# Slots of a sparse edge bucket given out from both ends, in a four-layer graph network on one core

## The chip, the core and the metric

The kernel runs on one NeuronCore of one Trainium2 chip. Its time is the device time of one launch, in microseconds (us); the time before is the median of three runs. One more execution was recorded by the hardware profiler, and every duration below is from that one.

A core has TensorE (PE, matrix products into PSUM), VectorE (DVE), ScalarE (ACT), GpSimd (POOL) and SyncE (SP). Each works through its own list of instructions in a fixed order and waits for the others by semaphores. SP computes nothing here: it issues the kernel's transfers (DMAs).

## The reference

Sixteen graphs of 1024 nodes with 128 features go through four residual layers, each of which starts with a layer norm and a ReLU. The adjacency is sparse and its pattern symmetric: an entry is there with a chance of about 1.6%, and the diagonal is full. Layers 0 and 1 are a mean over neighbours and a linear map; layer 3 is an attention over the neighbours. The change is in layer 2, which runs two rounds of this:

```python
a = jnp.einsum('bnd,de->bne', x, We1[l, :D])
b = jnp.einsum('bnd,de->bne', x, We1[l, D:])
h = jax.nn.relu(a[:, :, None, :] + b[:, None, :, :] + be1[l])
scores = jax.nn.sigmoid(jnp.squeeze(h @ We2[l], -1) + be2[l])
upd_adj = adjacency * scores
messages = jnp.einsum('bnm,bmd->bnd', upd_adj, x)
```

A score is needed for each pair of nodes (n, m), but it counts only where the adjacency isn't zero.

## The kernel before, in words

**Buckets.** The kernel computes h only for the pairs that are edges. The 1024 nodes are eight blocks of 128. A bucket is the set of edges between block t and block u: 28 outer buckets (t < u) and 8 on the diagonal. Each edge of a bucket gets a slot. An outer bucket has `C_OFF` = 320 slots, a diagonal one `C_DIAG` = 480. Slots are given out in the order of the row nodes: node 0's edges first, then node 1's, and so on. If a bucket has more edges than slots, a flag is raised and a general path (`Pairs`) computes everything anew at the end.

**Selection matrices.** For each bucket `build` makes four matrices of zeros and ones in an 8-bit format: `on` (row node x slot), `om` (column node x slot) and their transposes `onT` and `omT` (slot x node, in chunks of 128 slots; the third chunk of an outer bucket has only 64 new slots). `rows_hot` makes `on`: ACT takes the distance of each slot number from the middle of the node's stretch (`far`), DVE compares it with half the stretch's width. `turned` transposes it on PE, ACT copies the result (`onT`). `omT` comes from a product of `on` with the ranks of the edges (`pq`) and a comparison on DVE; `turned_back` and a copy on ACT give `om`. `count` has made the starts and widths from the row sums, with a triangular matrix `low2`.

**One round of layer 2** (`round`) goes through nine groups of four buckets: the first four diagonal buckets, seven groups of outer ones, the last four diagonal ones. An outer bucket is done in both directions (d = 0, 1), since the edge (n, m) and the edge (m, n) have different scores. For each group:

- `split` has computed a and b for every node, as 16-bit numbers in two parts, the rounded value and what is left (`part`).
- `gather` (line 1051) brings them to the slots: the products of `part` with `on` and with `om`, each for both parts, add up in the PSUM bank `pre`. That is four matmuls for each bucket and direction. There are two `pre` banks. ACT takes the ReLU (`hid`, line 1068), DVE the remainder (line 1069).
- `dots` (line 1091) makes the product of `hid` with the signs of We2: one score for each slot, with the slots on the partitions (`sc`). `ends` takes the tanh (line 1107).
- `scores` multiplies the scores onto `onT` (direction 0) or `omT` (direction 1), for two buckets at a time (`val`, DVE, line 1140). Each number of `val` is a pair of 16-bit halves.
- `scatter` (line 1165) brings the scores to a 128 x 128 block of the adjacency: `omT` or `onT` as stationary operand, the halves of `val` as moving one, five matmuls for an outer bucket and direction, eight for a diagonal bucket. It is issued in four parts behind the gathers of the next group. DVE multiplies with the adjacency (`upd`, line 1173), and PE adds up the messages (line 195).

**The order of the work.** The program weaves three lanes: `main` (layer 2 of batch b), `first` (layers 0 and 1 of batch b+1 and then its `build`), and `last` (layer 3 of batch b-1). Each lane yields an estimate of the time of what it has issued, and `weave` takes next the lane with the least share of its total (`MAIN_US` = 184, `FIRST_US`, `LAST_US`). A tile scheduler then lays down each engine's order at build time. Buffers come from pools that rotate: `hot` holds the selection matrices of one batch and two outer buckets more; lane m has five scratch tiles (`N_SCRATCH`).

**SP's queue** holds all transfers in one order: the adjacency for each group (`adj`, issued by `load_adj`), strips of it for layer 3 (`a`), the loads and stores of layers 0 and 1 (`at`, `ct`, `l`, `adjT`), and copies of features (`xm`, `xTk`, `xT`). A transfer whose buffer is still in use stops all that stand behind it.

## Time and profile before

| what | value |
|---|---|
| median of three runs (lowest to highest) | 5286.28 us (5273.41 to 5290.21) |
| the profiled execution's own time | 5291.36 us |
| its span, first to last instruction | 5289.5 us |
| mean granted TensorE clock | 0.977 |
| busy: PE, DVE, ACT | 4904.9, 4207.7, 2954.9 us |
| bytes moved by DMAs | 555.46 MB, mean 105 GB/s |
| SP's queue: share of 16 DMA engines | 34.1% |

A row of the groups reads: line, engine, operation, what it writes and what it reads, its shape (partitions x elements), how many, then the busy time in us with overlaps counted once, the mean of one in ns, and the engine's idle time just before such instructions with what ended it. Matmuls overlap one another, so count times mean is more than their busy time. PEld is the loading of a stationary operand. The chain that ended last is followed back from the last instruction, at each step to what released it.

### The profile page before, as it was taken

The page shows a single profiled execution, that of the slowest core. Times are in us where ns is not written, and L with a number is a line of the kernel's source. Part 1 is how long each engine was busy: PE and PEld are TensorE (multiplying, and loading weights), DVE is VectorE, ACT ScalarE, POOL GpSimd, SP SyncE. Part 2 cuts the span into 40 slices and gives each one's busy share as a digit, 9 for nine tenths or more (in the row PEclk, how much of TensorE's full clock was granted, in tenths as well). Part 3 has the DMA queues.
Part 4 walks back from the last instruction along what each step waited for, and adds up shares of the span by engine and source line. Part 5 has one row for each costly group of instructions (what it writes and reads, how often), then busy time and mean ns, then how long its engine had stood idle before and what let it go on. Part 6 is the DMA issues. An engine that isn't in the chain of part 4 may idle for free.

```text
span 5289.5 us, 127581 instructions
## 1 busy us (share of the span) xinstructions
PE 4904.9 (93%) x52773; PEld 3883.7 (73%) x52773; DVE 4207.7 (80%) x9543; ACT 2954.9 (56%) x6566; POOL 176.2 (3%) x137
## 2 busy tenths in 40 slices
PE   6999999999999999999999999999999999999986
PEld 5777777777777777777777777777777777777665
DVE  4777787977879788797877878778797887978876
ACT  5556564655646556464555646556465564655533
POOL 0000000000000000000000000000000000000000
PEclk8999999999999999999999999999999999999998
DMA  6343325243342433424233152432524334243121
GB/s 186 91 120 115 103 78 151 69 137 96 91 147 69 126 98 108 131 62 138 90 117 119 59 155 79 131 106 79 152 68 138 94 98 140 69 124 95 56 68 48
DMA packets 740189, 555.46 MB, mean 105 GB/s; under 512 B 32272, under 2 KB 686352, under 8 KB 739600
## 3 DMA queue, kind: packets, MB, share of 16 engines
q1 hardware_dynamic: 734496, 545.58, 34.1%
q8 instruction: 416, 6.82, 0.5%
q10 hardware_dynamic: 5104, 1.65, 0.1%
q14 instruction: 173, 1.42, 0.1%
HBM read 446.44 MB, written 100.66 MB: 103 GB/s over the span
## 4 chain that ended last, share of the span: by engine, by line
PE 54%; DVE 26%; ACT 9%; DMA 6%; POOL 3%; issue 3%; SPq 0%; ACTq 0%; DVEq 0%; POOLq 0%
PE pre L1051 13%; DVE val L1140 7%; PE p L1165 6%; PE nb L301 5%; PE sc L1091 5%; PE msg L195 5%; DVE hid L1069 4%; DMA at<-in_adj_dram 3%; PE bb L309 3%; PE hp L195 3%; PE h L355 3%; PE pq L910 2%; DMA a<-adjT 2%; PE pn L853 2%; DVE omT L913 2%
## 5 line engine op out<-in xcount | busy, mean ns | idle before, releaser
L1068 ACT ACTIVATE hid<-pre 128x320 f16<-128x320 f32 (+1 forms) x2048 | 914.6, 451 | 837.4 <-PE pre L1051 779.9
L1069 DVE SCALAR_TENSOR_TENSOR hid<-pre,hid 128x320 f16<-128x320 f32 (+1 forms) x2048 | 1010.6, 506 | 216.2 <-ACT hid L1068 198.3
L1051 PE MATMUL pre<-on,part 128*128 128x320 fp8e4 (+1 forms) x4096 | 973.1, 310 | 30.7 <-DVE hid L1069 25.0
L1051 PE MATMUL pre<-om,part 128*128 128x320 fp8e4 (+1 forms) x4096 | 978.5, 310 | 0.0
L1051 PEld LDWEIGHTS <-part 128*128 128x128 f16 x8192 | 748.2, 98 | 298.3 <-issue 82.8
L195 PE MATMUL msg<-upd,xf 128*128 128x128 f32 (+3 forms) x3008 | 597.6, 324 | 0.4 <-DVE upd L1173 0.3
L1140 DVE TENSOR_TENSOR val<-onT,u 128x768 f32<-128x768 fp8e4 (+1 forms) x576 | 572.4, 1011 | 3.3
L1165 PE MATMUL p<-val,omT 128*128 128x128 f16 x6528 | 501.9, 218 | 21.2 <-DVE val L1140 17.0
L1165 PEld LDWEIGHTS <-omT 128*128 128x128 fp8e4 x6528 | 420.4, 96 | 72.0 <-issue 30.5
L1091 PEld LDWEIGHTS <-hid 128*128 128x128 f16 x12800 | 378.5, 96 | 64.6 <-DVE hid L1069 44.9
L195 PEld LDWEIGHTS msg<-upd,xf 128*128 128x128 f32 x3008 | 405.5, 191 | 21.9 <-DVE upd L1173 12.1
L1140 DVE TENSOR_TENSOR val<-omT,u 128x768 f32<-128x768 fp8e4 x448 | 411.1, 951 | 0.0
L1091 PE MATMUL sc<-slide,hid 128*128 128x1 f16 x12800 | 399.0, 163 | 11.1 <-DVE hid L1069 8.0
L1173 DVE SCALAR_TENSOR_TENSOR upd<-p,adj 128x512 f32<-128x512 f32 x512 | 349.8, 683 | 63.3 <-PE p L1165 60.8
L921 ACT ACTIVATE om<-pm 128x320 fp8e4<-128x320 f32 (+1 forms) x576 | 267.3, 464 | 205.6 <-PE pm L866 202.4
L1165 PE MATMUL p<-val,onT 128*128 128x128 f16 x4480 | 359.4, 220 | 1.5 <-DVE upd L1173 1.3
L906 ACT ACTIVATE onT<-pn 128x384 fp8e4<-128x384 f32 (+1 forms) x576 | 294.8, 512 | 110.9 <-PE pn L853 104.0
L195 PE MATMUL hp<-wh,e 128*128 128x129 f32 x2048 | 317.3, 287 | 13.9 <-DVE e L523 13.8
L1165 PEld LDWEIGHTS <-onT 128*128 128x128 fp8e4 x4480 | 298.5, 97 | 32.5 <-issue 3.6
L195 PEld LDWEIGHTS hp<-wh,e 128*128 128x128 f32 x2048 | 271.8, 196 | 28.5 <-DVE e L523 11.8
L301 PE MATMUL nb<-z,ct 128*128 128x128 f32 x2048 | 271.0, 285 | 22.7 <-ACT tn L771 20.3
L913 DVE TENSOR_TENSOR omT<-pq,odd_off 128x384 fp8e4<-128x384 f32 x448 | 248.8, 555 | 47.8 <-PE pq L910 39.9
(212 smaller groups left out, 7839.7 us busy)
## 6 DMA issues: line engine op xcount, KB each, us to landing
at<-in_adj_dram SPq DMA_DIRECT2D x128, 512.0 KB, 4.0
ct<-in_adj_dram SPq DMA_DIRECT2D x128, 512.0 KB, 4.4
adjT<-tn SPq DMA_DIRECT2D x128, 512.0 KB, 4.9
l<-adjT SPq DMA_DIRECT2D x128, 512.0 KB, 4.4
adj<-adjT SPq DMA_DIRECT2D x256, 256.0 KB, 3.6
a<-adjT SPq DMA_DIRECT2D x128, 384.0 KB, 3.3
adj<-adjT SPq DMA_DIRECT2D x448, 64.0 KB, 2.1
adj<-adjT SPq DMA_DIRECT2D x192, 128.0 KB, 2.7
```

The source lines that it names most:

```text
L195: ins = nc.tensor.matmul(dst, left, right, start=opened is None, stop=True, skip_group_check=True)
L301: nc.tensor.matmul(ps, mat[:, k], z[:, k], start=(k == 0), stop=(k == T - 1))
L906: nc.scalar.activation(onT, pn[:, : ck * P], AF.Copy, saturate=False)
L913: nc.vector.tensor_tensor(omT.rearrange("p (k m) -> p k m", m=P), pq[:, :ck], self.odd[t == u][:, :, None].to_broadcast([P, ck, P]), op=OP ...
L921: nc.scalar.activation(om, pm[:, :c], AF.Copy, saturate=False)
L1051: ins = nc.tensor.matmul(pre[:, :c], path.parts[node // Q][:, k, node % Q, v], hot[:, :c], start=(hot is on and k == 0), stop=(hot is om a ...
L1068: nc.scalar.activation(hid[:, 0, :c], pre[:, :c], AF.Relu)
L1069: nc.vector.scalar_tensor_tensor(hid[:, 1, :c], pre[:, :c], 0.0, hid[:, 0, :c], op0=OP.max, op1=OP.subtract)
L1091: ins = nc.tensor.matmul(self.sc[:, k, j : j + 1], self.hid[j][:, v, at : at + P], sign, start=self.open is None, stop=True, skip_group_ch ...
L1140: nc.vector.tensor_tensor(pair[:, :, :ck], right, v.rearrange("p k i o -> p i k o").to_broadcast([P, 2, ck, P]), op=OP.mult,)
L1165: nc.tensor.matmul(self.ps[d][:, i], left[:, k], halves[:, k, :, h], start=(k, h) == terms[0], stop=(k, h) == terms[-1],)
L1173: nc.vector.scalar_tensor_tensor(upd, self.ps[d], S_SCALE, self.adj[:, d * Q : (d + 1) * Q], op0=OP.add, op1=OP.mult,)
```

## The change

**Slots from both ends.** The row nodes of a bucket are halved. Nodes 0 to 63 (the front) get slots from 0 upwards, nodes 64 to 127 (the back) from the last slot downwards. A half may use `REACH_OFF` = 176 slots of an outer bucket, `REACH_DIAG` = 256 of a diagonal one; the flag is raised if a half or a whole bucket has more.

**Gather.** `twice` copies the front rows of `on` with their 176 slots, and the back rows with theirs, onto both halves of the partitions of a tile `st`: four DMAs of 64 partitions for each bucket, on SP's queue. `split` likewise makes a tile `both`, in which the 64 front nodes have the rounded value on partitions 0 to 63 and the remainder on 64 to 127, and the same for the back nodes: four DMAs for each half of the blocks. One matmul of 128 partitions then does both parts of 64 nodes. The two matmuls of `on` with all slots become two of `st` with 176 (256) slots; those of `om` stay, and go first.

**Build.** An outer bucket's `onT` has 256 columns in place of 384: 64 for the first 128 slots and the front nodes, 64 for the last 128 slots and the back nodes, 128 for the 64 slots in the middle (twice, on both halves of the partitions) and all nodes. It is kept for the four buckets of a group in one tile, no longer in pairs, and `omT` for each bucket by itself. `on` has four rotating buffers.

**Scores and scatter.** In `ends` an outer group's tanh is written by two instructions, the second reading the last chunk twice. For outer groups `val` holds four chunks of 64 nodes, for four buckets at once, and is made from `onT` in both directions. Direction 0's scatter is one matmul of 128 and four of 64 columns. Direction 1 takes 64 columns of `val` as the stationary operand and `omT` as the moving one: six matmuls of 128 columns that fill 64 output partitions each. An outer group is scattered in three parts: two buckets of direction 0, the other two, all four of direction 1.

Other edits: lane m has four scratch tiles, and the ranks' copy adds a bias for each half.

```diff
-N_SCRATCH = {"m": 5, "a": 4, "c": 5}
+N_SCRATCH = {"m": 4, "a": 4, "c": 5}
+N_ON = 4
...
+        def twice(self, on, t, u, name):
+
+            n, back = reach(t, u)
+            st = self.hot_tile("st", t, u, 2 * n, name)
+            for first, rows in ((0, slice(0, HP)), (back, slice(HP, P))):
+                at = n if first else 0
+                for to in (slice(0, HP), slice(HP, P)):
+                    nc.sync.dma_start(st[to, at : at + n], on[rows, first : first + n])
+            return st
+
+        def slots_down(self, on, diag, name):
 
             ps = self.a.one(name)
-            for k, at in enumerate(hot_at(ck)):
+            if diag:
+                parts = [(k * P, at, 0, P) for k, at in enumerate(HOT_AT[True])]
+            else:
+                a, b, c = HOT_AT[False]
+                parts = [(0, a, 0, HP), (HP, b, HP, HP), (P, c, 0, P)]
+            for to, at, first, n in parts:
                 nc.tensor.matmul(
-                    ps[:, k * P : (k + 1) * P], hot[:, at : at + P], self.eye16,
+                    ps[:, to : to + n], on[:, at : at + P], self.eye16[:, first : first + n],
                     start=True, stop=True,
                 )
...
+            front, back = slice(0, HP), slice(HP, P)
+            for rows, k in ((front, 0), (back, 1)):
+                nc.sync.dma_start(both[front, k], parts[rows, k])
+                nc.sync.dma_start(both[back, k], parts[rows, 1 - k])
...
-                    parts.extend((old, part) for part in range(Q))
+                    parts.extend((old, part) for part in range(old.pieces))
...
-                    for v, node, hot in ((d, t, on), (1 - d, u, om)):
-                        for k in range(2):
-                            ins = nc.tensor.matmul(
-                                pre[:, :c], path.parts[node // Q][:, k, node % Q, v], hot[:, :c],
-                                start=(hot is on and k == 0),
-                                stop=(hot is om and k == 1),
-                            )
+                    parts, _ = path.parts[u // Q]
+                    for k in range(2):
+                        nc.tensor.matmul(
+                            pre[:, :c], parts[:, k, u % Q, 1 - d], om,
+                            start=(k == 0), stop=True, skip_group_check=True,
+                        )
+                    _, both = path.parts[t // Q]
+                    for k, at in enumerate((0, c - n)):
+                        ins = nc.tensor.matmul(
+                            pre[:, at : at + n], both[:, k, t % Q, d], st[:, k * n : (k + 1) * n],
+                            start=False, stop=True, skip_group_check=True,
+                        )
...
-                nd = self.nd
+                nd, each, onT = self.nd, 2 if self.diag else Q, self.s.onT[self.k]
                 for d in range(nd):
-                    for i in range(0, Q, 2):
+                    for i in range(0, Q, each):
...
+                    if self.diag:
+                        terms = [
+                            (ps[:, i], omT[:, k], halves[:, k, :, h])
+                            for k in range(self.ck) for h in (1, 0)
+                        ]
+                    else:
+                        halves = halves.rearrange("p c n h -> p (c n) h")
+                        a, b = slice(0, HP), slice(HP, P)
+                        seen = [(2, halves[:, P + sl.start : P + sl.stop, 1], sl) for sl in (a, b)]
+                        seen += [
+                            (k, halves[:, sl, h], sl) for h in (1, 0) for k, sl in enumerate((a, b))
+                        ]
+                        if d:
+                            terms = [(ps[sl, i], v, omT[:, k]) for k, v, sl in seen]
+                        else:
+                            terms = [(ps[:, i, sl], omT[:, k], v) for k, v, sl in seen[2:]]
+                            terms.insert(0, (ps[:, i], omT[:, 2], halves[:, P:, 1]))
```

## The prediction, made before the changed kernel ran

> **What bounds the kernel now.** I read the page first, then the groups with shapes kept apart, the time line of PE, and the waits of SP's queue. Totals and the chain that ended last:
>
> ```profile
> PE 4904.9 (93%) x52773; PEld 3883.7 (73%) x52773; DVE 4207.7 (80%) x9543; ACT 2954.9 (56%) x6566; POOL 176.2 (3%) x137
> PE 54%; DVE 26%; ACT 9%; DMA 6%; POOL 3%; issue 3%; SPq 0%; ACTq 0%; DVEq 0%; POOLq 0%
> PE pre L1051 13%; DVE val L1140 7%; PE p L1165 6%; PE nb L301 5%; PE sc L1091 5%; PE msg L195 5%; DVE hid L1069 4%; DMA at<-in_adj_dram 3%; PE bb L309 3%; PE hp L195 3%; PE h L355 3%; PE pq L910 2%; DMA a<-adjT 2%; PE pn L853 2%; DVE omT L913 2%
> ```
>
> PE leads, DVE follows; the three costliest items of the chain (pre, val, p) are the ones that the diff edits. The groups:
>
> ```profile
> L1051 PE MATMUL pre<-om,part 128*128 128x320 fp8e4 x3584 | 829.8, 301 | 0.0
> L1051 PE MATMUL pre<-on,part 128*128 128x480 fp8e4 x512 | 156.0, 366 | 7.7 <-DVE hid L1069 6.2 <-DVE part L938 1.2
> L1165 PE MATMUL p<-val,omT 128*128 128x128 f16 x6528 | 501.9, 218 | 21.2 <-DVE val L1140 17.0 <-DVE upd L1173 2.6
> L1165 PE MATMUL p<-val,onT 128*128 128x128 f16 x4480 | 359.4, 220 | 1.5 <-DVE upd L1173 1.3
> L1140 DVE TENSOR_TENSOR val<-onT,u 128x768 f32<-128x768 fp8e4 x448 | 417.9, 951 | 2.7
> L1140 DVE TENSOR_TENSOR val<-omT,u 128x768 f32<-128x768 fp8e4 x448 | 411.1, 951 | 0.0
> L1140 DVE TENSOR_TENSOR val<-onT,u 128x1024 f32<-128x1024 fp8e4 x128 | 154.5, 1219 | 0.6
> L906 ACT ACTIVATE onT<-pn 128x384 fp8e4<-128x384 f32 x448 | 218.6, 488 | 87.7 <-PE pn L853 81.5 <-PE p L1165 1.0
> L1107 ACT ACTIVATE tan<-sc,be_s,down 128x24 f32<-128x24 f32 x224 | 83.1, 371 | 102.1 <-PE sc L1091 96.5
> ```
>
> A matmul's mean holds its pipeline's length. What it takes from PE is the distance between starts: in the time line (start, length, count) the length of a run less one mean, over count less one.
>
> ```profile
> 2607.15 0.90 PE L1165 MATMUL p<-val,omT 128*128 128x128 f16 x13
> 2621.20 0.43 PE L1051 MATMUL pre<-on,part 128*128 128x320 fp8e4 x2
> 2621.47 0.43 PE L1051 MATMUL pre<-om,part 128*128 128x320 fp8e4 x2
> 2625.85 0.74 PE L1091 MATMUL sc<-slide,hid 128*128 128x1 f16 x24
> ```
>
> 128 columns: (0.90-0.22)/12 = 57 ns. 320: two starts in 0.27 us, 136 ns. One column: (0.74-0.16)/23 = 25 ns. The same reading gives 202 ns at 480 and 112 ns for a float32 matmul of 128 columns. Count times distance over all groups is about 4,530 us, of which pre is 7168 x 0.136 + 1024 x 0.202 = 1,182 and p 11008 x 0.057 = 627. So PE streams for 86% of the span, and what it stops doing should come back for the most part.
>
> SP's queue, waits and issues:
>
> ```profile
> SPq L1027 <- DVE upd L1173: 1076.9, 202, 31.3
> SPq L1257 <- DVE e L523: 862.4, 121, 43.3
> 2850.21 1.88 SPq L1027 DMA_DIRECT2D adj<-adjT  x4
> ```
>
> It stands mostly behind an adjacency row or a strip that DVE hasn't freed; an issue costs it 0.3 to 0.47 us (1.88/4).
>
> **What the Trainium skill says.** "TensorE: Matmul & The Clock Gate", section "Back-to-back issue gap": N/2.4 + 2.5 ns, about 60 cycles at least; the trace agrees (136 at 320, 202 at 480, 57 at 128, 25 at 1). "TensorEngine Tiling (Array Packing)", "Key Properties": half-array tiles load and multiply in parallel, but a change of tiling mode drains the array; "Feature Incompatibilities": column tiling excludes fast weight load. The trace has no 64-column tile, so neither is shown. "DMA: Bandwidth & Descriptors", "Rules for kernel authors": transfers to disjoint partition halves serialize. No DMA of this trace writes half the partitions.
>
> **The change, part by part.**
>
> *Gather.* Per outer bucket and direction, 4 x 320 columns become 2 x 320 + 2 x 176. Between 57 (128) and 136 (320) a column costs 0.41 ns, so 176 costs 76 ns and 256 costs 110. Outer: 1792 x 2 x (136-76) = -215 us; diagonal: 256 x 2 x (202-110) = -47. Sum -262. om now goes before the half rows; both are ready, so this is nothing in itself.
>
> *Scatter, direction 0.* Five 128-column matmuls (285 ns) become one of 128 and four of 64 (57 + 4 x 31 = 181): 896 x -104 = -93 us.
>
> *Scatter, direction 1.* Five become six that fill half the output columns, with 64 columns of val as weights and omT moving. Not shown by the trace. If halves a and b run together: 3 x 57 = 171, 896 x -114 = -102 us. One after the other: 6 x 57 = 342, +51 us. Upper end: weights not hidden (64/1.2 = 53 ns by the first page's section "LDWEIGHTS"), 6 x 110 = 660, +336 us; and a drain into and out of each run: this group's 4480 matmuls come in 631 runs now, 1,262 changes; at the page's 398 cycles (0.166 us) +209 at most. I take +51 and a fifth of the drains, +42: the parts a and b alternate, so loads can hide, but nothing here shows two running together.
>
> *Build.* pn loses one 128-column matmul in effect (two of 128 become two of 64): 448 x 2 x -26 = -23 us on PE. onT 384 to 256 columns: 488 to 382 ns (0.83 ns a column, from om's 435 at 320), ACT -47 us. way2 for low2, rank with a bias, count's few small operations: 16 or 144 times nearly the same instruction; nothing, beside 5,000 us of PE.
>
> *val.* 896 x 0.951 = 852 us of outer multiplies become 448 x 1.219 = 546: DVE -306 us.
>
> *ends.* A second tanh for each outer group: 224 x 0.36 = +80 us of ACT, at 56%, so hidden; but scores start 0.36 us later, with other lanes' work beside it. If bare: +80.
>
> *New DMAs on SP.* 576 buckets x 4 + 64 halves x 4 = 2,560 issues, at 0.43 us some 1,100 us of a queue that now has about 1,850 issues and waits over 4,000 us. Each `on` now has one of 4 buffers and is freed only by its copies' landing (smallest shown: 64 KB, 2.1 us). Covered: three further buckets are built in between. If the cover is gone DVE waits in rows_hot, with hid, val and upd of the other lanes behind it. `both` isn't covered by its own lane: gathers start about 2 x 0.43 + 2.1 = 3 us (four issues and SP's queue: 4 us) after the last part, three times a batch, 48 x 3.5 = 168 us raw. Beside it nb, hp and h run on PE (at 2854 to 2860 PE is busy all 6.00 us), so I charge a quarter: +42.
>
> *Buffers.* Group m's scratch goes from 5 to 4, while val needs 2 for an outer group in place of 4: nothing. Three parts per outer group in place of four end its last upd before the next group starts: SP's wait on upd may shorten; no credit. The same step takes 14 x 0.6 = 8.4 off main's yields, which make up about 186 against MAIN_US of 184: main is emitted 4% ahead, and the other lanes end each batch alone. The next batch's first groups can run beside them, so nothing; bare, 4% of 330 us a batch at a third idle, 16 x 4 = 70 us.
>
> *Sum on PE:* -262 - 93 + 51 + 42 - 23 = -285. By the chain instead: pre 13% (688 us) x -22% = -151, val 7% (370) x -31% = -115, p 6% (317) x 0% = 0 (-93 + 93), pn 2% (106) x -32% = -34: -300. They agree; I take -292 + 42 for `both` = -250. The profiled execution took 5291.4 us (span 5289.5), so 5041, 5 us less against the median 5286: **5040 us**.
>
> **Rivals.**
> 1. *Halves run together* (-102 in place of +93): 195 less on PE, 160 of it kept: 4880. For: a and b alternate in the diff. Against: changes of mode between the lanes' matmuls.
> 2. *The gain turns into waits.* A gather then takes 2 x 136 + 2 x 76 = 424 ns of PE, below ACT's 435 and DVE's 485 for the same hid; with two pre banks PE waits for them. A third of the gain remains: 5200. For: ACT and DVE wait in the profile for each other at hid (198 us). Against: val frees 306 us of DVE, and two other lanes fill PE.
> 3. *Slower: direction 1 pays the upper end.* If loads aren't hidden and each run drains, +336 + 209 in place of +93 is 452 more: -250 + 452 = +202; two thirds of that beyond zero, where loads hide in part: 5430. It decides once a half-array matmul takes about 105 ns (57 + 250/5.376) in place of 57. For: the page's exclusion of fast loads. Against: float32 matmuls, whose loads last 191 ns in the groups, still start 112 ns apart.
> 4. *Slower: the copies sit behind SP's waits.* 0.55 us of DVE at each of 576 buckets, +317: 5360. For: waits up to 43 us. Against: DMAs queued behind belong to later work.
> 5. *Buckets overflow a half's reach* and the general path runs as well: a half of 64 x 128 holds 127 expected slots at density 0.0156, deviation 11; 176 is over 4 away, the diagonal's 256 likewise. Under 1 in 100.
>
> **How the numbers follow.** Forecast 0.48 (own range 4950 to 5150), rival 1 0.11, rival 2 0.16, rival 3 0.16, rival 4 0.09. Within 0.3% (16 us, what a measurement can tell here): 0.04, from the edge of rivals 2 and 4. Faster: 0.48 + 0.11 + 0.13 = 0.72; slower 0.24. The range 4880 to 5390 leaves out the lower half of rival 1 and the upper parts of 3 and 4, about 0.19.
>
> **What would show it.** pre: half the matmuls at 176 and 256 columns, starts 76 and 110 ns apart. p: 64-column forms 31 ns apart; half-array ones, starts 57 (forecast), under 30 (rival 1), over 100 (rival 3). val: 448 outer at 1.22 us, DVE near 3,900 us. SP: about 4,400 issues; waits of `on` for DMAs under 100 us in all, else rival 4; pre waiting for `both` under 60 us. hid waits above 400 us would be rival 2. A slower kernel with short p distances and short DMA waits would refute all of it: then the order of the instructions has moved.

## The result, and the profile after

The kernel after takes 5322.50 us (median of five runs, 5316.77 to 5332.04), the kernel before 5286.28 (5273.41 to 5293.09 in its five). The ratio is 1.0072, with a 95% interval of 1.0052 to 1.0092: **36 us slower**, where 246 us faster was forecast. The profiled execution took 5316.77 us, with a span of 5314.9 and a mean granted TensorE clock of 0.940 (before: 0.977).

The page of the kernel after, busy times and the chain that ended last:

```profile
PE 4662.6 (88%) x53685; PEld 3708.6 (70%) x53685; DVE 3928.4 (74%) x9128; ACT 2945.6 (55%) x6790; POOL 172.9 (3%) x137
PE 52%; DVE 21%; ACT 10%; DMA 9%; issue 4%; SPq 2%; POOL 2%; DVEq 0%; ACTq 0%; POOLq 0%
PE nb L306 6%; PE pre L1113 6%; PE p L1257 6%; PE msg L200 6%; DVE val L1212 5%; PE sc L1158 4%; PE bb L314 4%; DVE hid L1136 3%; PE pre L1119 3%; DMA a<-adjT 3%; PE h L360 3%; DMA at<-in_adj_dram 2%; SPq L892 2%; PE xn L369 2%; PE pq L962 2%
```

Every engine has less to do: PE 242 us less, DVE 279, ACT 9. Still the span has grown by 25. On the chain, pre fell from 13% to 9% and val from 7% to 5%, as meant. DMAs rose from 6% to 9%, and SP's queue, which had no share at all, now holds 2%, all of it line 892, the new copies. So the work was saved, and waiting took its place.

The groups, with shapes kept apart:

```profile
L1113 PE MATMUL pre<-om,part 128*128 128x320 fp8e4 x3584 | 821.8, 308 | 71.9 <-DVE hid L1136 68.5
L1119 PE MATMUL pre<-st,both 128*128 128x176 fp8e4 x3584 | 599.7, 245 | 0.0
L1119 PE MATMUL pre<-st,both 128*128 128x256 fp8e4 x512 | 105.5, 273 | 20.2 <-DMA both<-part 20.1
L1257 PE MATMUL p<-val,omT 128*128 128x64 f16 x3584 | 203.2, 192 | 0.0
L1257 PE MATMUL p<-omT,val 128*64 128x128 fp8e4 x5376 | 258.8, 234 | 2.4 <-DVE upd L1264 2.3
L1212 DVE TENSOR_TENSOR val<-onT,u 128x1024 f32<-128x1024 fp8e4 x576 | 687.3, 1218 | 2.0
L880 DVE TENSOR_SCALAR on<-far,wid 128x384 fp8e4<-128x384 f16 x448 | 183.8, 413 | 11.4 <-DMA st<-on 6.4 <-PE pn L904 1.7 <-ACT onT L958 1.5
```

Two things are to be seen. Each operation is there in the number and size forecast. And the waits that carry the name of a new copy are small: 6.4 us for a free `on` of an outer bucket, 20.1 for `both` on PE. If one looked for the loss under the names of the new transfers alone, one would not find it.

A stretch of the time line of PE in direction 1 (start, length, operation, count) shows how the half-array matmuls run:

```profile
2928.22 0.32 PE L1119 MATMUL pre<-st,both 128*128 128x176 fp8e4 x2
2928.46 0.24 PE L1257 MATMUL p<-omT,val 128*64 128x128 fp8e4 x1
2928.64 0.40 PE L962 MATMUL pq<-rank,on 128*128 128x128 f16 x4
2928.97 0.87 PE L1257 MATMUL p<-omT,val 128*64 128x128 fp8e4 x23
2929.76 0.91 PE L200 MATMUL msg<-upd,xf 128*128 128x384 f32 x2
```

By the prediction's reading, (0.87 - 0.234)/22 = 29 ns from start to start: half of what one full 128-column matmul takes. In the single records they come in pairs, 4 to 6 ns apart, and then 52 ns to the next pair. Two halves do run at once. Changing to them and back does cost. The second 176-column matmul starts at 2928.22 + 0.32 - 0.245 = 2928.295, and the half-array one 0.165 us later, not 0.076; the last of the 23 starts at 2929.606, and the full one after it 0.154 us later, not 0.052. Over all 448 runs of such matmuls the medians are 93 ns extra on the way in and 99 on the way out, 86 us in all.

**Where a batch ends.** One batch takes as long after as before, but in other parts. The table is worked out from the records of `hid` and of the copy that writes `om`: medians over ten batches, in us from the first `hid` of the batch's layer 2 to the start of the one named (a round ends with its last `hid` on DVE). "Last om" is the last step of the next batch's `build`, without which its layer 2 can't go on; the next batch's first `hid` comes at "period".

| kernel | round 0 ends | round 1 starts | round 1 ends | first om | last om | period |
|---|---|---|---|---|---|---|
| before | 140.7 | 160.1 | 301.5 | 188.1 | 328.9 | 322.4 |
| after | 128.8 | 151.1 | 289.1 | 187.2 | 325.9 | 323.3 |

Layer 2 of a batch has become 12 us shorter (301.5 to 289.1). The `build` of the next batch ends where it did, at 326 to 329. So the 12 us are not saved; they become a longer tail in which `build` runs with little beside it. The busy times of one batch, by stretch (round 0 with what precedes round 1, round 1, and from there to the next batch's first `hid`; columns: stretch, length, then busy time and count of PE, PEld, DVE, ACT and POOL, granted clock, DMA share, GB/s). Before:

```profile
3022.90:3183.10 160.20, 154.62 (x1622) 126.01 (x1621) 118.12 (x280) 76.48 (x167) 6.35 (x5) 0.99 0.48 143
3183.10:3324.80 141.70, 130.78 (x1489) 100.82 (x1488) 128.93 (x278) 94.74 (x216) 2.94 (x2) 0.98 0.22 69
3324.80:3345.70 20.90, 18.87 (x192) 14.39 (x189) 14.78 (x38) 13.09 (x29) 1.64 (x1) 1.00 0.30 93
```

After:

```profile
3052.70:3203.40 150.70, 143.95 (x1642) 118.26 (x1640) 111.35 (x273) 79.58 (x178) 6.29 (x5) 0.99 0.54 159
3203.40:3341.20 137.80, 119.16 (x1489) 92.82 (x1490) 113.73 (x248) 84.91 (x207) 2.64 (x2) 0.92 0.29 81
3341.20:3377.20 36.00, 29.90 (x232) 22.86 (x231) 19.72 (x48) 19.20 (x43) 1.64 (x1) 0.72 0.37 96
```

The last row is where the saving goes: 36.0 us in place of 20.9, at a clock of 0.72 in place of 1.00. In the mean of twelve batches this stretch is 32.6 us at 0.81, against 20.3 at 1.00. ACT's time line there shows `build` going bucket by bucket, each copy waiting for PE's transposes (the bracket is the idle time ahead of it and what ended that):

```profile
3364.91 0.57 ACT L973 ACTIVATE om<-pm 128x480 fp8e4<-128x480 f32 x1 [4.03 <-PE pm L919]
3370.65 0.57 ACT L973 ACTIVATE om<-pm 128x480 fp8e4<-128x480 f32 x1 [2.40 <-PE pm L919]
3374.49 0.57 ACT L973 ACTIVATE om<-pm 128x480 fp8e4<-128x480 f32 x1 [0.70 <-PE pm L919]
3376.58 0.56 ACT L1135 ACTIVATE hid<-pre 128x480 f16<-128x480 f32 x1
```

**The first two batches.** Thirteen batches in the middle take as long as before, so the 36 us must lie elsewhere. In the profiled executions, in us, counted from the first `hid` of each batch:

| kernel | batches 0 and 1 | batches 2 to 14 | batch 15 to the end |
|---|---|---|---|
| before | 634.9 | 4193.2 | 335.9 |
| after | 673.6 | 4187.6 | 327.8 |

The first two are 39 us longer, more than the whole loss. Before batch 1's layer 2 can start, SP's queue after holds this (start, length, count), and PE starts right behind it:

```profile
414.84 59.65 SPq L892 DMA_DIRECT2D st<-on  x92
474.54 0.59 SPq L997 DMA_DIRECT2D both<-part  x1
475.18 0.59 SPq L998 DMA_DIRECT2D both<-part  x1
477.64 0.37 PE L1119 MATMUL pre<-st,both 128*128 128x256 fp8e4 x1 [0.26 <-DMA both<-part]
```

For 60 us SP issues 92 copies of `st` and nothing else. The `both` that the first gathers need stands behind them. PE has little but `build` to do meanwhile, so it is seldom idle for long, and the wait under the name of `both` is 0.26 us.

**A third place**, at the end of round 0, where layer 2's features are transposed for round 1. The time line of PE after:

```profile
4827.06 0.43 PE L1113 MATMUL pre<-om,part 128*128 128x320 fp8e4 x2
4827.33 0.31 PE L1119 MATMUL pre<-st,both 128*128 128x176 fp8e4 x2
4827.48 0.87 PE L200 MATMUL hp<-wh,e 128*128 128x129 f32 x6
4834.45 0.90 PE L1305 MATMUL tp<-ident,xf 128*128 128x128 f32 x3 [6.10 <-DVE xf L388]
4836.29 0.74 PE L1113 MATMUL pre<-om,part 128*128 128x320 fp8e4 x2
4836.82 0.50 PE L1119 MATMUL pre<-st,both 128*128 128x176 fp8e4 x2
```

PE stands for 6.10 us behind DVE's layer norm, and what follows runs at half the clock: the pair of 320-column matmuls takes 0.74 us in place of 0.43. The same place before:

```profile
4813.84 1.12 PE L1214 MATMUL tp<-ident,xf 128*128 128x128 f32 x4 [1.66 <-DVE xf L383]
```

The clock is at half here too: four such transposes take 0.66 us at full rate (in the last lines of the section on the clock), and 1.12 here. What differs is how long it lasts. The stretches that the clock records give as half rate, before and then after (columns as above):

```profile
4813.22:4816.63 3.41, 2.79 (x16) 2.52 (x17) 3.11 (x6) 1.62 (x5) 0.00 (x0) 0.50 0.55 220
4832.15:4845.80 13.65, 10.64 (x76) 7.87 (x77) 7.68 (x23) 7.81 (x21) 1.64 (x1) 0.50 0.30 101
```

In all, PE waits there 14 times for 6.10 us, 85 us in sum. The clock in the records is either full or half, so its mean gives the time at half rate: 2 x (1 - 0.940) x 5315 = 638 us, against 2 x (1 - 0.977) x 5290 = 243 before (the records themselves sum to 642 and 250).

So there were four suspects: the copies on SP's queue, the transfers of `both`, the pace of the three lanes (the yields of `main` are fewer, `MAIN_US` is the same), and the clock. The experiments take them in turn.

### The profile page after: what moved, and what is told of

Same layout as the page of the kernel before. It is cut to its first block, busy times and chain, and to the rows that moved or that the text cites. A ratio compares the mean times of both kernels' runs of the same rounds, so it can differ in the third digit from the quotient of the medians.

```text
span 5314.9 us, 133237 instructions
## 1 busy us (share of the span) xinstructions
PE 4662.6 (88%) x53685; PEld 3708.6 (70%) x53685; DVE 3928.4 (74%) x9128; ACT 2945.6 (55%) x6790; POOL 172.9 (3%) x137
## 4 chain that ended last, share of the span: by engine, by line
PE 52%; DVE 21%; ACT 10%; DMA 9%; issue 4%; SPq 2%; POOL 2%; DVEq 0%; ACTq 0%; POOLq 0%
PE nb L306 6%; PE pre L1113 6%; PE p L1257 6%; PE msg L200 6%; DVE val L1212 5%; PE sc L1158 4%; PE bb L314 4%; DVE hid L1136 3%; PE pre L1119 3%; DMA a<-adjT 3%; PE h L360 3%; DMA at<-in_adj_dram 2%; SPq L892 2%; PE xn L369 2%; PE pq L962 2%
## 5 line engine op out<-in xcount | busy, mean ns | idle before, releaser
L1119 PE MATMUL pre<-st,both 128*128 128x176 fp8e4 (+1 forms) x4096 | 705.1, 248 | 20.2 <-DMA both<-part 20.1
L1212 DVE TENSOR_TENSOR val<-onT,u 128x1024 f32<-128x1024 fp8e4 x576 | 687.3, 1218 | 2.0
L200 PE MATMUL msg<-upd,xf 128*128 128x128 f32 (+3 forms) x3008 | 640.5, 335 | 11.6 <-DVE upd L1264 11.5
L1119 PEld LDWEIGHTS <-both 128*128 128x128 f16 x4096 | 397.7, 100 | 202.5 <-DMA both<-part 30.3
L1113 PEld LDWEIGHTS <-part 128*128 128x128 f16 x4096 | 360.0, 100 | 161.8 <-issue 130.9
L1257 PE MATMUL p<-val,omT 128*128 128x64 f16 (+1 forms) x6528 | 378.5, 205 | 47.4 <-DVE val L1212 46.1
L1257 PEld LDWEIGHTS <-omT 128*128 128x128 fp8e4 x6528 | 333.6, 97 | 84.6 <-issue 60.2
L958 ACT ACTIVATE onT<-pn 128x256 fp8e4<-128x256 f32 (+1 forms) x576 | 246.9, 429 | 117.1 <-PE pn L904 104.8
L876 ACT ACTIVATE far<-iota_off,mid 128x384 f16<-128x384 f16 x448 | 273.7, 615 | 26.3 <-DVE on L880 22.6
L919 PE MATMUL pm<-eye,omT 128*128 128x128 f16 (+1 forms) x1856 | 199.3, 224 | 93.5 <-DVE omT L966 91.3
```

The costliest lines, as they stand in the source:

```text
L200: ins = nc.tensor.matmul(dst, left, right, start=opened is None, stop=True, skip_group_check=True)
L876: nc.scalar.activation(far[:, :n], self.iota[t == u][:, :n], AF.Abs, bias=s.mid[:, i : i + 1])
L1113: nc.tensor.matmul(pre[:, :c], parts[:, k, u % Q, 1 - d], om, start=(k == 0), stop=True, skip_group_check=True,)
L1119: ins = nc.tensor.matmul(pre[:, at : at + n], both[:, k, t % Q, d], st[:, k * n : (k + 1) * n], start=False, stop=True, skip_group_check=True,
L1212: nc.vector.tensor_tensor(val, onT[:, i : i + each].rearrange("p i (c n) -> p i c n", n=n), v.rearrange("p k i o -> p i k o").to_broadcast ...
L1257: nc.tensor.matmul(dst, left, right, start=n < first, stop=True, skip_group_check=True)
```

## The experiments

Each kernel is a small edit of the kernel after, unless it says otherwise. All times are medians; the ratio is to the kernel before, run beside it on the same chip. There the kernel before took 5278.6 to 5288.6 us, so the difference of two medians from different chips is good to about 10 us.

### Which part costs: scatter alone, no copies, no `both`

`scatter_alone` keeps the new slots, `val` and scatter, and gathers from whole rows of `on` and from `part`, without `st` and `both`. An outer bucket's rows are read in two pieces, of 192 and 128 slots.

```diff
-            on = self.work.tile([P, HALF], FP8, tag="on", ..., bufs=N_ON)[:, :n]
+            on = self.hot_tile("on", t, u, n, name)
...
-                    s.st[t, u] = self.twice(on, t, u, nm)
+                    s.st[t, u] = on
...
+                    cuts = [(0, 0, c)] if self.diag else [(0, 0, P + HP), (P + HP, 2 * P, P)]
+                    for k in range(2):
+                        for at, first, n in cuts:
+                            ins = nc.tensor.matmul(
+                                pre[:, at : at + n], rows[:, k, t % Q, d], st[:, first : first + n], ...
```

> The changed kernel with the gather of before: `on` with all its slots (320 columns, in two pieces of 192 and 128) kept for the whole batch, no copies of its rows and no `both`. Slots from both ends, the new val and the new scatter stay. If the copies and the waits that they bring eat the gain, this one has a gain: val's 306 us of DVE and 140 us of PE less than before, 5150 to 5230. If PE and DVE time was never what sets the end of a batch, it stays at 5270 to 5320. If the scatter's new form itself loses time, above 5330.

Measured: 5220.7 us, ratio 0.9870 (0.9850 to 0.9891).

`no_copies` gathers from one tile of zeros, so the 2,304 copies of `st` and the 256 of `both` are gone while every matmul stays. The row nodes' share of the result is left out.

```diff
-            st = self.hot_tile("st", t, u, 2 * n, name)
-            for first, rows in ((0, slice(0, HP)), (back, slice(HP, P))):
...
-            return st
+            return self.st0[:, : 2 * n]
...
-            self.parts[h] = parts, both
+            self.parts[h] = parts, parts
```

> The changed kernel without its 2,560 new DMAs: the half rows are read from one constant tile of zeros, `part` stands in for `both` (the share of the row nodes is left out of the sums; every matmul, activation and vector operation stays in number and shape). If the copies (SP's queue, four `on` buffers, the wait of the first gathers of a round) cost what the change was to gain, 5020 to 5150. If they cost only the waits that the trace puts down to them by name (20 us on PE, 6 on DVE), 5270 to 5320: then the order or the lanes' balance is the cause.

Measured: 5113.2 us, ratio 0.9673 (0.9657 to 0.9689).

`no_both` keeps the copies of `st`, and reads `part` where `both` was read; its sums mix the wrong halves.

> Only the 256 DMAs of `both` are gone, `part` is read in its place (sums are wrong by that); the 2,304 copies of `on` stay. If the start of a round is what lost the time (the first gathers come 3 to 4 us later, three times a batch): 48 x 3.5 = 168 us less, 5130 to 5180. If not, 5290 to 5330.

Measured: 5267.2 us, ratio 0.9962 (0.9949 to 0.9974), between the two ranges expected.

**What follows.** All new DMAs together cost 209 us (5322.5 - 5113.2). Without those of `both` alone the kernel is 55 us faster. In the profiled executions that is 47 us, of which 29 lie in batches 0 and 1 (644.8 us in place of 673.6) and only 8 in batches 2 to 14. Batch 0 alone falls from 352.2 us to 285.7 (287.6 before): it was `both`, in its place in the queue, that held batch 1 back. So `both` costs little three times a batch, as was expected of it; it costs where it stands behind the copies of `st`, and its 55 us can't be parted from theirs. The cost is of the transfers and not of the new matmuls. `scatter_alone` is faster than the kernel after by 102 us: as the kernel after stands, the half rows lose more by their copies than they save. But even without any copy the gain is 173 us, short of 246. In `no_copies` the last om still comes at 320.1, 33 us after round 1's end at 286.7 (27 us before), but the next batch's layer 2 starts earlier: the stretch between is 24.1 us in the mean, no longer 32.6.

### The pace of the lanes

Added up over a middle batch, the yields of `main` come to 183.8 in the kernel before and to 175.4 in the kernel after, 8.4 fewer. (The prediction's "about 186" was near the former.) Those of `first` come to 116.7 of its 118 in both. So before, `main` ended at 183.8/184 = 1.00 of its total, when `first`, at 116.7/118 = 0.99, was done. After, it ends at 175.4/184 = 0.95, and `first` then has 4% of 118, some 4 units, to issue without layer 2 beside it: close to the last group of `build`, whose four diagonal buckets yield 5.1. The three `om` copies of 480 columns in ACT's time line above are of that group. With 176 the share is 175.4/176 = 1.00 again. A lane whose steps count for more is taken later, so `first` with its `build` moves forward.

```diff
-MAIN_US = 184.0
+MAIN_US = 176.0
```

> The changed kernel with MAIN_US at 176 in place of 184, which matches the 8.4 that main no longer yields. If the lanes fall out of step (main through its batch 4% early, the others then alone, PE at half clock there), the 6.1 us pause of PE in each batch goes and 50 to 150 us come back: 5170 to 5270. If balance isn't it, 5300 to 5340.

Measured for `main176`: 5172.4 us, ratio 0.9786 (0.9770 to 0.9802). This one number takes 150 us off the kernel after. In the profiled executions 134 of 143 us come off batches 2 to 14; batches 0 and 1 stay long, at 669.6.

To see whether 176 is simply the better number, the kernel before got it too:

> The kernel before with MAIN_US at 176 and nothing else. If the pause at the batch's end comes from the change's shorter account of main (8.4 fewer units), this puts the lanes of before out of step the other way: 5290 to 5400. If 176 is simply the better number for any of these kernels, it is 2 to 3% faster than before, 5130 to 5190, and the change has no part in that gain.

Measured for `before_176`: 5312.4 us, ratio 1.0069 (1.0052 to 1.0087): slower. And one step further on the changed kernel, 168:

> The changed kernel with MAIN_US at 168. If the balance follows main's yields (177.6), 176 is about right and this is slower again: 5190 to 5280. If it follows the real time, of which main has lost more (PE 285 us and DVE 306 us less, all in main's groups), it is faster still: 5100 to 5160.

Measured for `main168`: 5238.2 us, ratio 0.9923 (0.9906 to 0.9940).

The table of the batch, continued:

| kernel | round 0 ends | round 1 starts | round 1 ends | first om | last om | period |
|---|---|---|---|---|---|---|
| after (184) | 128.8 | 151.1 | 289.1 | 187.2 | 325.9 | 323.3 |
| main176 | 127.7 | 149.6 | 287.0 | 174.4 | 312.7 | 312.0 |
| main168 | 125.1 | 150.8 | 294.1 | 174.0 | 317.3 | 316.8 |
| before_176 | 145.5 | 164.5 | 306.5 | 194.6 | 332.3 | 323.0 |

With 176 the rounds end where they did, within 2 us, and `build` starts and ends 13 us sooner; the tail shrinks. With 168 the first om comes no earlier than with 176 (174.0 against 174.4), and round 1 ends 7 us later. The selection matrices have buffers for one batch and two outer buckets more, so most of a batch's are written only when round 1 of the batch before has read the old ones; that this is what holds the first om at 174 is argued from the code, not shown by a run of its own. In the kernel before, 176 makes the share 183.8/176 = 1.04, and both the rounds and `build` come later; in the changed kernel 168 makes it 175.4/168 = 1.04, and it is slower than 176. So each kernel was fastest, of the values tried, where the share is 1.00: the number goes with the sum of the yields. Raising the yields in place of lowering the number was not tried.

The tail of the same kind of batch in `main176`, same view as above:

```profile
3275.70:3299.30 23.60, 22.24 (x218) 16.02 (x219) 15.27 (x41) 14.72 (x32) 1.73 (x2) 1.00 0.44 124
```

23.6 us at full clock, in place of 36.0 at 0.72. In the mean of twelve batches it is 24.2 us at 0.97, in place of 32.6 at 0.81: two thirds of the way back to the 20.3 of before.

### What of a copy costs: SP's queue or its landing

With the pace mended, three ways to do the copies, and one without the half rows. `half_176` lets GpSimd copy those two of four pieces that stay on their own partitions; two DMAs for each bucket stay on SP.

```diff
+                    if to == rows:
+                        nc.gpsimd.tensor_copy(st[to, at : at + n], on[rows, first : first + n])
+                    else:
+                        nc.sync.dma_start(st[to, at : at + n], on[rows, first : first + n])
-                    nc.sync.dma_start(st[to, at : at + n], on[rows, first : first + n])
```

> MAIN_US 176, and of the four copies of a bucket two are made by GpSimd (those that stay on their own partitions), so SP issues 1,152 DMAs less; the result is the reference's. If SP's issues (0.4 to 0.65 us each) and what queues behind them are the copies' cost, half of the way from main176 (5172) to the kernel without copies comes back: 5070 to 5130. If the cost is that a buffer of `on` comes back only when its copies have landed (two DMAs still have to), under 30 us: 5140 to 5180.

Measured: **5024.4 us**, ratio 0.9516 (0.9499 to 0.9533). It beats both kernels, and by more than either range expected.

`pool_176` leaves all four DMAs as they are and issues them from GpSimd's queue in place of SP's (`nc.gpsimd.dma_start`).

> MAIN_US 176 and all four copies of a bucket issued from GpSimd's queue, none from SP's. The copies and their landing times stay. If what they cost is SP's queue (their own 0.4 to 0.7 us each, and strips and adjacency rows behind them), 5020 to 5080, as in half_176. If it is the landing of the copies before `on` comes back, 5150 to 5200.

Measured: 5063.0 us, ratio 0.9584 (0.9562 to 0.9607).

`no_copies_176` and `scatter_176` are the two kernels of the first section with 176.

> Both at once: no new DMAs (the row nodes' share left out of the sums as before) and MAIN_US 176. If the copies (200 us) and the lanes' balance (150 us) are separate losses, they add up: 4950 to 5000. If they are one loss seen twice (both make the other lanes late at a batch's end), it ends where no_copies does: 5090 to 5120.

Measured: 5057.8 us, ratio 0.9573 (0.9550 to 0.9597), between the two ranges: neither "separate" nor "one loss".

> The gather of before with the new val and scatter, at MAIN_US 176. At 184 it took 5221. If the 6 us pause in it is the same fault of balance as in the changed kernel, 5100 to 5150 (80 to 120 less). The difference to half_176 (5024) is then what the half rows bring once their copies are cheap: 215 us of PE, of which 80 to 120 us arrive.

Measured: 5178.9 us, ratio 0.9801 (0.9784 to 0.9819). That is 42 us less than at 184, where 80 to 120 were expected.

`half_184` is `half_176` with the pace left alone.

> The changed kernel with MAIN_US 184 as it is, and two of the four copies of each bucket made by GpSimd. From no_copies (200 us less than after at 184) and half_176 (148 less than main176): 5110 to 5180 if copies and balance are separate; above 5250 if the copies only matter once the lanes are balanced.

Measured: 5189.4 us, ratio 0.9816 (0.9795 to 0.9838), 9 us above the range for "separate".

**What follows.** `pool_176` moves the same bytes, in as many DMAs, to the same places, and is 109 us faster than `main176`, though a copy now lands 2.26 us after its issue in the median, in place of 1.81. Without any copy the kernel is 115 us faster (`no_copies_176`). So most of what the copies cost is the place that they take in SP's queue, not their landing. Nor do they slow the other transfers once issued: the 64 KB rows of `adj` land after 2.1 us before and in `main176`, and after 2.3 in the kernel after. SP's time line in the kernel after shows what stands there (start, length, count):

```profile
4813.77 2.92 SPq L1348 DMA_DIRECT2D a<-adjT  x2
4816.78 6.12 SPq L892 DMA_DIRECT2D st<-on  x8
4822.95 1.64 SPq L1348 DMA_DIRECT2D a<-adjT  x2
4825.28 4.94 SPq L892 DMA_DIRECT2D st<-on  x8
4830.32 0.53 SPq L768 DMA_DIRECT2D xk<-x  x1
```

Eight copies take 4.9 to 6.1 us of the queue, and between two strips of layer 3's adjacency lie 6.2 us in which no other transfer can leave. Over the run the copies of `st` hold SP for 1,420 us (0.62 us each), those of `both` for 144. The queue paid with the time in which it had stood ahead of its work, as its waits after show (in us, times, longest):

```profile
SPq L1088 <- DVE upd L1264: 553.3, 143, 13.3
SPq L1348 <- DVE e L534: 299.0, 67, 41.7
SPq L892 <- DVE on L880: 193.7, 132, 4.4
```

The first two were 1,076.9 and 862.4 us before. A transfer that used to stand ready when its buffer came free is now issued later, and the wait is booked under that transfer's name. All waits of PE, DVE and ACT that a DMA ended sum to 163 us before, 223 after, 252 in `main176`, 200 in `pool_176` and 155 in `half_176`. In the kernel after, 109 of them stand under `a` (61 before), 20 under `both`, and 8 under `st`. Which one of them costs most was not tried apart, and these sums are not the whole loss: in the 60 us of the first two batches PE had work of `build`, and hardly waited by name. In `half_176` SP holds 1,152 copies for 650 us, and the chain shows no share of SP's queue again:

```profile
PE 51%; DVE 26%; ACT 10%; DMA 7%; issue 4%; POOL 2%; SPq 0%; DVEq 0%; POOLq 0%; ACTq 0%
L893 POOL COPY st<-on 64x176 fp8e4<-64x176 fp8e4 (+1 forms) x1152 | 458.5, 398 | 1951.9 <-PE pre L1122 511.6
```

GpSimd, idle for 97% before, does its half in 458 us.

The 60 us in which SP issues only copies are gone too: batches 0 and 1 take 626.8 us in `half_176` and 625.0 in `pool_176`, against 669.6 in `main176`.

**Do the two causes add up?** With half of the copies, yes: from the kernel after, the pace alone gives -150 and the lighter queue alone -133 (`half_184`), which makes -283; both together give -298. With no copies they don't: -150 and -209 would make -359, and `no_copies_176` has -265. Put otherwise, 176 is worth 150 or 165 us where DMAs on SP copy the half rows (after, `half_184`), and 55 or 42 where none do (`no_copies`, `scatter_alone`), though all four have the same yields of `main`. In those two the tail is short already at 184, 24.1 and 23.3 us in the mean. So the long tail of the kernel after comes of the pace and the queue together, and its loss can't be divided between them.

`no_copies_176` does less than `half_176`, and is 33 us slower. Nothing on record explains that. Each edit also changes the order that the scheduler lays down for the rest, and no run shows what that alone is worth; so differences of this size are not read as causes here. Against `scatter_176` the half rows now bring 155 us, where in the kernel after they lost 102.

### The clock

`fill` is the kernel after, with 24 matmuls of 512 columns on constants put ahead of the transposes at which PE stood for 6.1 us, once a batch. What they write is overwritten.

```diff
             ps = lane.one(f"tp_{name}").rearrange("p (t d) -> p t d", d=P)
+            for _ in range(24 if h else 0):
+                nc.tensor.matmul(
+                    flat(ps), self.eye16, self.iota2, start=True, stop=True, skip_group_check=True
+                )
```

> The changed kernel with 24 matmuls of 512 columns on constants put into PE's order just ahead of the transposes at which PE stands still for 6.1 us in each batch (5.2 us of work at full clock, 15 times; their result is overwritten). They change no wait. If the half clock after the pause costs time of its own, the 6 to 14 us at half clock that follow each pause go and 40 to 80 us come back: 5240 to 5280. If the batch's end hangs on another chain, nothing changes or up to 40 us are lost: 5310 to 5360.

Measured: 5252.0 us, ratio 0.9933 (0.9912 to 0.9954).

```profile
4771.95 5.34 PE L1305 MATMUL tp<-iota,eye 128*128 128x512 f16 x24
4779.90 0.66 PE L1309 MATMUL tp<-ident,xf 128*128 128x128 f32 x4 [1.03 <-DVE xf L388]
```

Useless work of 16 x 5.3 = 86 us was added, and the kernel got 70 us faster. The mean clock rose from 0.940 to 0.958, that is from 638 to 441 us at half rate; 197 us at half rate hold at most some 98 us of lost work. The four transposes take 0.66 us here, where three took 0.90.

But the time isn't gained where the pause was. By the means over twelve batches, round 1, in which the pause lies, takes 137.4 us in place of 138.2, although its time at half rate falls from 15.5 to 7.4 us. The stretch behind it falls from 32.6 to 29.1 us, and its clock rises from 0.81 to 0.90. The order of PE's other matmuls differs too: in a stretch of 6000 of them, only 70% line up with the kernel after. So `fill` shows that less time at half rate and a faster kernel came together; how much of the 70 us is the clock and how much the order stays open.

The Trainium skill has a rule under "TensorE: Matmul & The Clock Gate", section "HAM oscillation — how this bites in real kernels": a wait longer than the monitor's window of about 3.4 us sends the clock to half, and the next stretch of work starts slow. The kernel after agrees: each of the 14 pauses of 6.10 us has a stretch at half rate of 6.8 to 13.7 us around its end. The kernel before shows that a shorter pause is no safeguard: of its 15 pauses of 1.2 to 1.7 us at the same place, 12 have one too, of 3.4 to 6.8 us. What sets the other three apart isn't known. The clock needs no cure of its own: `main176` has 424 us at half rate (0.959) and `half_176` 301 (0.970), without any filler.

## Why the prediction was wrong

The sign was wrong by two steps that the sum set to nothing. The operations themselves came out as priced, with one exception in favour of the change.

- *Gather, -262 us.* Right. In the start records 176 columns lie 76 ns apart, 256 columns 109 (forecast 76 and 110), 320 still 136.
- *Scatter, direction 0, -93 us.* Right: 29 ns for 64 columns, 31 forecast.
- *Scatter, direction 1, +93 us (51 for serial halves, 42 for drains).* Both terms mis-sized, in the change's favour on balance. The halves run together, as rival 1 had it: 155 us lie between the starts within the runs, and 448 x 0.052 = 23 behind their last ones. The drains, of which the prediction took a fifth (42 us), come to 86. That makes 264 us, against 4,480 x 0.057 = 255 before: +9 in place of +93. The prediction took "nothing here shows two running together" for an answer. The Trainium skill has one, on "TensorE: Matmul & The Clock Gate", section "Measured speedup vs the span model": column tiles overlap, with about 4 ns for each further one. The pairs 4 to 6 ns apart agree, and the 93 and 99 ns agree in kind with the drain that the prediction cited. The 166 ns that it took as the upper end for a drain are, where it found them, the constant in the latency of a single matmul. Weight loads of 64 columns last 116 ns in the groups, and matmuls 29 ns apart show that they hide.
- *val, -306 us of DVE; build; ends.* Right: 448 outer products and the 128 of the diagonal at 1.218 us each, DVE at 3,928 us (about 3,900 forecast), onT at 382 ns as forecast. ACT, at 2,946 us, has no more to do than before; whether scores that start later cost anything isn't shown.
- *`both`, +42.* The size is near, 55 us by `no_both`, but by luck. The step laid the cost at three starts of gathers in each batch; of the 47 us in the profiled executions, 29 lie in batches 0 and 1, where `both` stands behind 92 copies of `st`. Its waits by name are 20.1 us on PE, below the 60 given.
- *"New DMAs on SP. ... Covered: three further buckets are built in between."* **The first step that failed.** The cover holds for the copy's own reader: DVE waits 8.2 us in all for `on`, against a limit of 100. It says nothing of the work queued behind on SP: `adj`, the strips, and `both`. Half of these copies on another engine is worth 133 us (184) or 148 us (176), and all of them on another queue 109 us (176). The issue was also under-priced, at 0.43 us against 0.62 measured. Rival 4 named this queue and priced it at +317. It had the roles the other way round: not the copies wait behind SP's other transfers, these wait behind the copies. So the waits of `on` that it asked for as its sign are not there. "DMAs queued behind belong to later work", which it gave against itself, is what failed at the start of batch 1.
- *"The same step takes 14 x 0.6 = 8.4 off main's yields ... so nothing; bare, 4% of 330 us a batch at a third idle, 16 x 4 = 70 us."* **The second step that failed:** 150 us by `main176`. The step saw the 4%, and took its cover (the next batch's first groups) from the wrong side. Those groups need the `build` that is late: emitted later, it ended later (last om 325.9 against 312.7 in `main176`), and the batch ended with it. Even the bare price of 70 us was half of what undoing it brings. The two steps are not separate: without copies the same 8.4 units cost 55 us, below the bare price.
- *The clock* has no step in the sum. Count times distance was worked out at full rate, and 395 us more at half rate (638 - 243) take back at most about half that, some 200 us of PE's saving. Most of it goes with the two failures above (`half_176` has 301 us at half rate), so it isn't added to them.

Rival 2 (waits in place of work) described best what PE did: DVE's wait for ACT at `hid` rose from 198 to 372 us, a little below the 400 that it asked for. But `hid` is not where the loss is cured: `half_176` wins 298 us with a wait of 327 us still there, so that rival's reason, ACT's 435 ns for each hid, is not what made the kernel slower. Rival 3 is refuted by the 29 ns, and rival 5 by the groups, which have no row of the general path. Rival 1 was right that the halves run together, but its gain of 195 us is 84 once the drains are counted in full, and it is not seen in the time. The prediction's last sentence held: slow, with short distances and short waits by name, means that the order has moved.

Put together: with both failed steps undone, the first in half, the kernel takes 5024.4 us, and the sum said 5040. Such closeness is partly luck, because direction 1 cost 84 us of PE less than the forecast counted, and nothing of that size shows in the time. How much of it was left at `hid`, and how much in the tail, stays open. The new gather alone, without the new scatter, was not tried.

## What to carry to other kernels

A kernel that weaves its lanes by estimates written into it has these estimates as part of every change: when a step is dropped, keep the ratio of a lane's yields to its total, or look first at what ends a batch last. Count the yields by program, not by head. A small transfer is priced twice, once at its reader and once in its queue, and the second price hardly bears its name. Count issues times issue time against the queue's slack, stretch by stretch, the start of the run included, and give the copies to an idle engine where the partitions allow. When all engines are less busy and the time is longer, look at the stretch in which only one lane runs, and at the clock there.

## What the runs showed of the hardware

- Two matmuls with 64-column weights that fill the two halves of the output partitions start 4 to 6 ns apart and then 52 ns to the next pair: 29 ns each on average, for 128 moving columns.
- A run of such matmuls costs PE 93 ns extra on the way in and 99 on the way out. A lane that slips one of them between the full matmuls of others, as in the time line above, pays 0.19 us for a matmul of 0.03; 448 runs of 12 on average came to 86 us.
- A DMA of 64 partitions with 176 or 256 bytes each, from SBUF to SBUF, holds SP for 0.62 us (0.56 in `half_176`), and lands in a median of 1.81 us. The 960 adjacency loads in the kernel before held it for 0.44 in the mean. Issued from GpSimd (`pool_176`), such a copy holds GpSimd for 0.53 us and lands in 2.26.
- GpSimd copies 64 x 176 8-bit numbers in 0.38 us, 64 x 256 in 0.46 (`half_176`).
- Pauses of PE of 1.2 to 1.7 us came with 3.4 to 6.8 us at half clock in 12 of 15 cases (before), those of 6.10 us with 6.8 to 13.7 us in 14 of 14 (after).
